# A state-space scan's sums: adding them to a PSUM bank that already holds the skip term

## The chip, the cores and the metric

The kernel runs on one core of one Trainium2 chip. Its time is the device time of one execution in microseconds (us), the median of several runs; the profile is of one further execution of the same program. A core has five engines, each of which works through its own instructions in program order: TensorE (PE, matmuls, with weight loads shown as PEld), VectorE (DVE), ScalarE (ACT), GpSimd (POOL) and SyncE (SP), which here only issues DMAs. Engines wait for each other through semaphores.

## The reference

The input is 8 images of 384 channels and 32 x 32 points. Layer 0 normalises each point, runs a Mamba block forwards and backwards over the 1024 points, and adds a gated depthwise convolution. Layer 1 is causal attention with 6 heads and a quantised feed-forward network with 1536 hidden units, applied to the first five images. What the change touches is the Mamba block's output, once for each direction:

```python
def step(h, inp):
    dA, dBu, c = inp
    h = dA * h + dBu
    return (h, jnp.einsum('bdn,bn->bd', h, c))
...
y = ys.transpose(1, 0, 2) + u * D_param
y = y * silu(z)
return jnp.einsum('bld,od->blo', y, out_proj_w)
...
g = (fwd + bwd) * scale_mod
```

Each channel has 16 states. The recurrence runs over the points; the states are weighted with C and summed, the skip term u D is added, and the result is gated with z. Gate and output projection are linear in y and the same for both directions, so the kernel adds the two directions' y first and gates and projects once.

## The kernel before, in words

**Recording and planning.** Every instruction is recorded as an `Op` with its tiles, and a planner (`Plan.place`) lays out the order of all engines with a list schedule: each operation has an assumed duration (`Plan.cost`), is ready when what it depends on has ended, and of the ready ones of an engine the one with the lowest rank goes first, if its tiles have a free buffer. Rank is the place in the recording, less what `hurry` takes off: 600 for all work of the scan, 60 more where a block says so. Operations in a `together` block stay adjacent. The resulting order is emitted as one fixed program per engine, so an edit in one place can move instructions everywhere. Since one helper emits everything, all of them carry line 367 in the profile, and are told apart by tile names.

**The scan.** A unit is (image b, part, channel chunk c of 128, state group j of 4, half q). The four parts of an image are (direction, half of the points) = (0,0), (0,1), (1,1), (1,0); the last image has the two directions exchanged. For each part and chunk there are 4 x 2 = 8 units, here called a group: 96 units an image, 768 in all, in 96 groups. In a unit the 128 partitions are 32 channels by 4 states, and it covers two such blocks of 512 points:

- `s_load`, `s_row`: SP loads delta (`scan_dl`), delta times u (`scan_ud`), and the rows B and C (`scan_bc`), from DRAM, broadcast over partitions.
- `s_first`: POOL makes `g = ud * B`, 128x1024, in one of six buffers (`scan_g`).
- `s_scan`: for each block ACT makes `da = exp(A dl)` in one of two PSUM banks (`ps_da`), DVE runs the recurrence over `g` in place (TENSOR_TENSOR_SCAN); the last column is kept for the next half by ACT (`scan_carry`); then POOL multiplies `g` by C in place.
- `s_sum`: for each pair of units (q = 0 and 1) four matmuls with the constant `gather` add up the 4 states of each channel and write 32 partitions each of the one PSUM bank `y` (`ps_y`). Four pairs make a group; the first starts the sum (`start=True`), the last ends it. When the pair's matmuls are done, its `g` buffers are free.
- `s_gate`: closes a group. SP loads u (`scan_us`). In the direction that comes first, DVE writes `yt = u D + y` to SBUF (`scan_yt`). In the second, DVE does three operations: `y = u D + y`, `y = yt + y`, `z = z y`, with z loaded into `scan_z`; SP writes the result to DRAM (`dram_sp_gy`), from where the attention reads it.

Units are shifted against each other: in the slot of unit k, `s_load` and the B rows are for unit k + 4, `s_first` for k + 2, `s_scan` for k, and `s_sum` and `s_gate` for k - 1.

**Beside the scan.** The steps of the other stages (`before_scan` of coming images, `attention` and the feed-forward network of finished ones) fill the other engines between the scan's slots, spread over them by assumed costs and due times. After the last unit only the second half of the last image's attention is left. `ident` is an identity matrix, `wproj` a weight of the attention, `vec` holds per-channel constants, D among them. PSUM has eight banks: one for `y`, two for `da`, five for everything else (`ps_any`).

Of the kernel before, what the change touches and what calls it, by code (L numbers as in the profile page):

```python
# [10 lines left out]
F32 = mybir.dt.float32  # L11
BF16 = mybir.dt.bfloat16
AF = mybir.ActivationFunctionType
ALU = mybir.AluOpType
# [4 lines left out]
P = 128  # L19
# [3 lines left out]
HB = 512  # L23
# [31 lines left out]
V_NORM, V_CW, V_CB, V_DTB, V_D, V_DW, V_DWB, V_BP, V_B2 = 0, 1, 5, 6, 7, 8, 17, 18, 19  # L55
# [105 lines left out]
class Plan:  # L161
# [15 lines left out]
    @contextmanager  # L177
    def together(self):
        self.group = []
        yield  # L180
        self.group = None

    @contextmanager
    def hurry(self, offset):
        self.sooner += offset
        yield
        self.sooner -= offset
# [193 lines left out]
def kernel(  # L381
# [21 lines left out]
    nc = plan = Plan(tc, homes)  # L403
    together, hurry = plan.together, plan.hurry
# [5 lines left out]
    sp = Pool(plan, "scan", 2, bass.MemoryType.SB)  # L410
# [3 lines left out]
    def ctile(name, shape, dt=F32):  # L414
        return const.tile(shape, dt, name=name, tag=name)
# [12 lines left out]
    def bank(name, tag=None):  # L428
        tag = tag if tag in BANKS else "any"
        return ps.tile([P, HB], F32, name=name, tag=tag, bufs=BANKS[tag])  # L430
# [4 lines left out]
    def half(h):  # L435
        return slice(h * HB, (h + 1) * HB)
# [4 lines left out]
    def load(dst, src):  # L441
        nc.sync.dma_start(out=dst, in_=src)
# [8 lines left out]
    spilled = {}  # L451
# [8 lines left out]
    vec = ctile("vec", [P, NC, NV])  # L460
# [8 lines left out]
    for d in range(2):  # L469
        nc.scalar.dma_start(out=wdt[d * DW : d * DW + RANK, :], in_=w_dt)  # L470
        nc.scalar.dma_start(
            out=wdt[d * DW + RANK : d * DW + RANK + 1, :],
# [10 lines left out]
    wproj = ctile("wproj", [P, NC, C])  # L483
    nc.scalar.dma_start(out=wproj, in_=w_proj.rearrange("(c p) e -> p c e", p=P))

    ident = ctile("ident", [P, P])
    make_identity(tc.nc, plan.now(ident))

    cmask = ctile("cmask", [P, HB], BF16)
    nc.vector.memset(cmask, 0.0)  # L490
# [468 lines left out]
    sst = {}  # L959
# [16 lines left out]
    def s_row(u, i):  # L976

        if u.c > 0 or u.q > 0:
            return
        r = sp.tile([P, HB], F32, name=f"bc{i}_{u.name}", tag=f"bc{i}", bufs=NG)  # L980
        rows = spilled[u.b, "rows", u.d][i * NS + u.j * SUB : i * NS + (u.j + 1) * SUB, half(u.h)]
        load(r, rows.partition_broadcast(BLK))
        sst["bc", i, u.b, u.part, u.j] = r
# [36 lines left out]
    def s_sum(u):  # L1020

        if u.q == 0:
            sst["pair"] = sst.pop(("g", u.name))
            return
        if u.j == u.first_group:
            sst["y"] = bank(f"y_{u.name}", "y")
        y = sst["y"]
        pair = (sst.pop("pair"), sst.pop(("g", u.name)))
        with together():
            for k in (2, 3, 0, 1):  # L1030
                nc.tensor.matmul(
                    out=y[k * BLK : (k + 1) * BLK, :],
                    lhsT=gather,
                    rhs=pair[k // 2][:, k % 2, :],
                    start=(u.j == u.first_group),
                    stop=(u.j == u.last_group),
                    skip_group_check=True,
                )

    def s_gate(u):  # L1040

        if not u.closes:
            return
        b, c, h, y = u.b, u.c, u.h, sst["y"]
        key = ("yt", b, c, h)
        t = sp.tile([P, HB], F32, name=f"uh_{u.name}", tag="us", bufs=1)
        load(t, spilled[b, "u", u.d, c][:, half(h)])
        if key not in sst:
            yt = sp.tile([P, HB], F32, name=f"yt_{u.name}", tag="yt", bufs=2 * NC)
            with hurry(offset=60):  # L1050
                nc.vector.scalar_tensor_tensor(
                    yt, t, vec[:, c, V_D : V_D + 1], y, ALU.mult, ALU.add
                )
            sst[key] = yt
            return
        z = sp.tile([P, HB], F32, name=f"zh_{u.name}", tag="z", bufs=1)
        load(z, spilled[b, "z", c][:, half(h)])
        yt = sst.pop(key)
        with hurry(offset=60):
            nc.vector.scalar_tensor_tensor(y, t, vec[:, c, V_D : V_D + 1], y, ALU.mult, ALU.add)  # L1060
            nc.vector.tensor_tensor(y, yt, y, ALU.add)
            nc.vector.tensor_tensor(z, z, y, ALU.mult)
        gy = dram.tile([P, HB], F32, name=f"sgy_{u.name}", tag=f"sp_gy_{c}_{h}")
        nc.sync.dma_start(out=gy, in_=z)
        spilled[b, "gy", c, h] = gy
# [440 lines left out]
    def slots(lo, hi):  # L1506
        def at(f, k):
            if 0 <= k < len(units):
                f(units[k])

        def slot(k):
            at(s_load, k + AHEAD + 2)
            at(lambda u: s_row(u, 0), k + AHEAD + 2)
            at(lambda u: s_row(u, 1), k + 2)
            at(s_first, k + AHEAD)
            at(s_scan, k)
            at(s_sum, k - 1)
            at(s_gate, k - 1)

        def ahead_of_all(k):  # L1520
            with hurry(offset=600):
                slot(k)

        return [(lambda k=k: ahead_of_all(k), 5.0) for k in range(lo, hi)]
# [62 lines left out]
    at = 0.0  # L1587
# [61 lines left out]
```

## Time and profile before

| what | value |
|---|---|
| time, median of 3 runs | 4044.43 us (4044.12 to 4044.86) |
| the profiled execution | 4048.24 us |
| its span, first to last instruction | 4046.4 us |
| TensorE's granted clock, mean over the span | 0.90 |
| busy: POOL, PE, DVE, ACT | 3570.8, 3387.3, 3264.4, 2546.6 us |
| first and last scan product on POOL start at | 74.8 and 3858.9 us |
| `ps_y` matmul records, DVE closings | 3072; 192 |
| ACT table loads | 131 |

The page is read as follows. The busy line gives each engine's busy time, its share of the span and its number of instruction records; an fp32 matmul is recorded as two. The slices cut the span into 40 equal parts of 101 us, and a digit is the busy share in tenths. A group's line has: source line, engine, operation, output tile <- input tiles, shape, xcount | busy us, mean ns of one | idle us of the engine just before them, and what ended that idle time. A line of waits reads: engine and what it was about to write <- whose end released it: us in total, times, the longest. A line of the timeline has start us, duration us, engine, operation, tiles, and in brackets the idle time before it. Buffer numbers are left out of names.

### The profile page before, as it was taken

The numbers are of one execution on the slowest core, as the hardware profiler recorded it, in microseconds if no ns is written. First come the engines' busy times: TensorE is split into PE (matmuls) and PEld (weight loads), VectorE is DVE, ScalarE is ACT, GpSimd is POOL, SyncE is SP. The second block draws the span as 40 slices with busy tenths as digits, with TensorE's granted clock in tenths as the row PEclk, the third lists the DMA queues.
The fourth block names the chain that finished last, engine by engine and source line by source line (L and its number), as shares of the span: only waits on it lengthen the run. The fifth ranks groups of instructions, "written<-read, shape, count | busy, mean of one in ns | idle before, by whom it ended". The sixth has DMA issues, their size and how long they took to land. (4 is left out here: it accounts for less than half of the span.)

```text
span 4046.4 us, 42961 instructions
## 1 busy us (share of the span) xinstructions
PE 3387.3 (84%) x12426; PEld 1330.0 (33%) x12426; DVE 3264.4 (81%) x4580; ACT 2546.6 (63%) x4967; POOL 3570.8 (88%) x1559
## 2 busy tenths in 40 slices
PE   5585679888699897998986989969989699898899
PEld 1121223333134332343332333323433233333344
DVE  5888987889977899678897687996779977778843
ACT  5666665866746766547667377664676654847635
POOL 2999999999999999789998799987899997999910
PEclk8685779899799898899997999979999799999999
DMA  7547655343563344742445533446334473333300
GB/s 237 194 141 242 235 191 174 100 144 126 202 209 124 102 147 135 247 157 86 134 161 195 183 110 105 138 169 242 123 100 138 142 266 127 113 122 108 128 16 32
DMA packets 338965, 611.99 MB, mean 151 GB/s; under 512 B 34616, under 2 KB 93416, under 8 KB 338728
## 3 DMA queue, kind: packets, MB, share of 16 engines
q1 hardware_dynamic: 329072, 593.10, 43.3%
q10 hardware_dynamic: 9656, 16.15, 1.2%
q8 instruction: 98, 1.61, 0.2%
q14 instruction: 139, 1.14, 0.1%
HBM read 456.03 MB, written 153.09 MB: 151 GB/s over the span
## 5 line engine op out<-in xcount | busy, mean ns | idle before, releaser
L367 POOL TENSOR_TENSOR scan_g<-scan_ud,scan_bc 128x1024 f32<-128x1024 f32 x768 | 1815.9, 2369 | 164.7 <-PE ps_y L367 97.0
L367 POOL TENSOR_TENSOR scan_g<-scan_g,scan_bc 128x1024 f32<-128x1024 f32 x768 | 1816.6, 2369 | 120.9 <-ACT scan_carry L367 66.0
L367 ACT ACTIVATE ps_da<-scan_dl,const_amat 128x512 f32<-128x512 f32 x1536 | 1052.6, 691 | 813.7 <-DVE scan_g L367 800.6
L367 DVE TENSOR_TENSOR_SCAN scan_g<-ps_da,scan_carry,scan_g 128x512 f32<-128x512 f32 x768 | 940.0, 1267 | 111.1 <-POOL scan_g L367 88.0
L367 PE MATMUL ps_any<-big_big,mid_mid 128*128 128x512 f32 x2016 | 952.9, 625 | 78.4 <-DVE big_big L367 56.5
L367 DVE TENSOR_TENSOR_SCAN scan_g<-ps_da,scan_g 128x512 f32<-128x512 f32 x768 | 893.1, 1206 | 127.8 <-POOL scan_g L367 86.9
L367 PE MATMUL ps_y<-scan_g,const_gather 128*32 128x512 f32 x3072 | 467.8, 686 | 275.1 <-POOL scan_g L367 265.0
L367 PEld LDWEIGHTS ps_any<-big_big,mid_mid 128*128 128x128 f32 x2016 | 388.0, 199 | 662.9 <-issue 486.3
L367 PE MATMUL ps_any<-big_big,big_big 128*128 128x512 f32 (+4 forms) x1728 | 551.9, 558 | 15.9 <-DVE small_nm L367 5.3
L367 PE MATMUL ps_any<-const_ident,mid_mid 128*128 128x128 f32 x1728 | 309.4, 304 | 96.0 <-DVE small_nm L367 44.1
L367 DVE CUSTOM_DVE_ANT_0 mid_mid<-ps_any,const_cmask 128x512 f32<-128x512 f32 (+3 forms) x576 | 291.2, 546 | 70.7 <-PE ps_any L367 69.7
L367 PEld LDWEIGHTS ps_any<-big_big,big_big 64*128 64x128 f32 (+1 forms) x1728 | 223.1, 189 | 309.9 <-issue 199.0
L367 DVE SCALAR_TENSOR_TENSOR ps_any<-big_big,const_vec,ps_any 128x496 f32<-128x496 f32 (+6 forms) x420 | 303.1, 727 | 21.6 <-ACT ps_any L367 11.9
L367 PEld LDWEIGHTS ps_any<-const_ident,mid_mid 128*128 128x128 f32 x1728 | 197.9, 149 | 331.2 <-DVE small_nm L367 100.3
L367 ACT COPY ptp_ptn<-ps_any 128x512 f32<-128x512 f32 (+3 forms) x576 | 255.2, 478 | 47.3 <-PE ps_any L367 38.4
L367 PE MATMUL ps_any<-ptp_ptn,big_big 128*64 128x512 f32 (+3 forms) x1152 | 262.3, 536 | 14.6 <-ACT ptp_ptn L367 13.1
L367 ACT ACTIVATE mid_mid<-mid_mid,small_low 128x512 f32<-128x512 f32 (+3 forms) x384 | 242.3, 634 | 47.5 <-DVE small_low L367 47.5
L367 PEld LDWEIGHTS ps_y<-scan_g,const_gather 128*32 128x32 f32 x3072 | 64.2, 114 | 545.0 <-POOL scan_g L367 443.6
L367 PE MATMUL ps_any<-mid_mid,const_onesc 128*128 128x512 f32 x252 | 131.2, 655 | 60.5 <-ACT mid_mid L367 45.6
L367 ACT ACT_TABLE_LOAD x131 | 168.1, 1283 | 2.9 <-PEq L1636 0.7
L367 PE MATMUL ps_any<-mid_mid,const_wdt 25*128 25x512 f32 x192 | 132.1, 852 | 41.6 <-DVE mid_mid L367 32.2
L367 DVE COPY big_big<-ps_any 128x512 f32<-128x512 f32 (+1 forms) x86 | 54.2, 631 | 128.6 <-PE ps_any L367 128.6
(100 smaller groups left out, 3185.4 us busy)
## 6 DMA issues: line engine op xcount, KB each, us to landing
scan_dl<-dram_sp_dl SPq DMA_DIRECT2D x384, 256.0 KB, 3.3
scan_ud<-dram_sp_ud SPq DMA_DIRECT2D x384, 256.0 KB, 3.7
scan_bc<-dram_rows SPq DMA_DIRECT2D x256, 256.0 KB, 3.4
scan_us<-dram_sp_u SPq DMA_DIRECT2D x96, 256.0 KB, 2.7
mid_mid<-dram_sp_u SPq DMA_DIRECT2D x96, 256.0 KB, 4.9
dram_sp_dl<-mid_mid SPq DMA_DIRECT2D x96, 256.0 KB, 4.0
dram_sp_ud<-mid_mid SPq DMA_DIRECT2D x96, 256.0 KB, 4.6
dram_sp_u<-mid_mid SPq DMA_DIRECT2D x42, 512.0 KB, 4.9
```

Source lines behind the costliest of these rows:

```text
L367: getattr(engine, what)(*[mapped(v) for v in args], **{k: mapped(v) for k, v in kwargs.items()})
```

## The change

The u load moves into a step of its own, `s_skip`, four units ahead of the scan, with two buffers in place of one. A new step `s_seed`, placed between `s_scan` and `s_sum`, takes the bank `y` and has ACT write `u D` to it; in the second direction DVE then adds `yt` to it in place. All sums are now accumulated on this content (`start=False`); a single matmul at the program's start writes the whole bank once, so that later matmuls without a start flag add to what is there. Closing a group is now one operation: in the first direction ACT copies `y` to `yt`, in the second DVE multiplies z by `y`.

```diff
+    nc.tensor.matmul(
+        out=bank("written", "y"),
+        lhsT=ident,
+        rhs=wproj.rearrange("p c e -> p (c e)")[:, :HB],
+        start=True,
+        stop=True,
+    )
...
-        if u.j == u.first_group:
-            sst["y"] = bank(f"y_{u.name}", "y")
...
-                    start=(u.j == u.first_group),
+                    start=False,
...
+    def s_skip(u):
+
+        if not u.opens:
+            return
+        t = sp.tile([P, HB], F32, name=f"uh_{u.name}", tag="us", bufs=2)
+        load(t, spilled[u.b, "u", u.d, u.c][:, half(u.h)])
+        sst["us", u.b, u.c, u.part] = t
+
+    def s_seed(u):
+
+        if not u.opens:
+            return
+        t, y = sst.pop(("us", u.b, u.c, u.part)), bank(f"y_{u.name}", "y")
+        yt, scale = sst.pop(("yt", u.b, u.c, u.h), None), vec[:, u.c, V_D : V_D + 1]
+        with hurry(offset=60):
+            nc.scalar.activation(y, t, AF.Copy, scale=scale)
+            if yt is not None:
+                nc.vector.tensor_tensor(y, yt, y, ALU.add)
+        sst["y"], sst["second"] = y, yt is not None
+
     def s_gate(u):
...
-        key = ("yt", b, c, h)
-        t = sp.tile([P, HB], F32, name=f"uh_{u.name}", tag="us", bufs=1)
-        load(t, spilled[b, "u", u.d, c][:, half(h)])
-        if key not in sst:
+        if not sst["second"]:
             yt = sp.tile([P, HB], F32, name=f"yt_{u.name}", tag="yt", bufs=2 * NC)
             with hurry(offset=60):
-                nc.vector.scalar_tensor_tensor(
-                    yt, t, vec[:, c, V_D : V_D + 1], y, ALU.mult, ALU.add
-                )
-            sst[key] = yt
+                nc.scalar.copy(yt, y)
+            sst["yt", b, c, h] = yt
             return
...
-        yt = sst.pop(key)
         with hurry(offset=60):
-            nc.vector.scalar_tensor_tensor(y, t, vec[:, c, V_D : V_D + 1], y, ALU.mult, ALU.add)
-            nc.vector.tensor_tensor(y, yt, y, ALU.add)
             nc.vector.tensor_tensor(z, z, y, ALU.mult)
...
             at(s_first, k + AHEAD)
+            at(s_skip, k + 4)
             at(s_scan, k)
+            at(s_seed, k - 1)
             at(s_sum, k - 1)
             at(s_gate, k - 1)
```

## The prediction

> **What bounds the kernel now.** First the page's busy times and its slices.
>
> ```profile
> PE 3387.3 (84%) x12426; PEld 1330.0 (33%) x12426; DVE 3264.4 (81%) x4580; ACT 2546.6 (63%) x4967; POOL 3570.8 (88%) x1559
> POOL 2999999999999999789998799987899997999910
> ```
>
> GpSimd (POOL) leads, and is full from its start at 74.8 us to the last scan unit at 3863 us; the head before and the tail after hold none of its work. Inside it is not full everywhere: the slices with 7 and 8 lie in the second half. So the span is head 75, POOL's work, POOL's waits, tail 183. Next the groups of instructions, each shape apart, for POOL and for what the change touches.
>
> ```profile
> L367 POOL TENSOR_TENSOR scan_g<-scan_ud,scan_bc 128x1024 f32<-128x1024 f32 x768 | 1815.9, 2369 | 164.7 <-PE ps_y L367 97.0 <-DMA scan_ud<-dram_sp_ud 61.5 <-issue 4.8
> L367 POOL TENSOR_TENSOR scan_g<-scan_g,scan_bc 128x1024 f32<-128x1024 f32 x768 | 1816.6, 2369 | 120.9 <-ACT scan_carry L367 66.0 <-DVE scan_g L367 42.6 <-issue 3.6
> L367 DVE SCALAR_TENSOR_TENSOR ps_y<-scan_us,const_vec,ps_y 128x512 f32<-128x512 f32 x48 | 35.9, 747 | 27.2 <-PE ps_y L367 27.0
> L367 DVE SCALAR_TENSOR_TENSOR scan_yt<-scan_us,const_vec,ps_y 128x512 f32<-128x512 f32 x48 | 35.5, 740 | 27.9 <-PE ps_y L367 27.7
> L367 DVE TENSOR_TENSOR ps_y<-scan_yt,ps_y 128x512 f32<-128x512 f32 x48 | 33.4, 696 | 1.6
> L367 DVE TENSOR_TENSOR scan_z<-scan_z,ps_y 128x512 f32<-128x512 f32 x48 | 33.0, 686 | 1.6
> L367 ACT ACTIVATE ps_any<-mid_mid,const_vec 128x512 f32<-128x512 f32 x60 | 40.9, 684 | 0.1
> L367 ACT COPY mid_mid<-ps_any 128x512 f32<-128x512 f32 x234 | 129.9, 584 | 36.8 <-PE ps_any L367 31.3 <-DVE mid_mid L367 3.6 <-DVE big_big L367 1.2
> ```
>
> A unit costs POOL 2 x 2.36 = 4.7 us and a group of eight 37.8 us; none of it is edited. What can move is its idle time of 285.5 us: 61.5 in the head, 224 inside. Of the inside, 97.0 is the first product waiting for a `g` buffer that TensorE's sums still hold; 66.0 and 42.6 are the second product waiting for carry or scan. The waits by stretch of POOL (75 to 1600 us, then 2150 to 2350 us) say where:
>
> ```profile
> POOL scan_g L367 <- PE ps_y L367: 3.4, 1, 3.4
> ...
> POOL scan_g L367 <- PE ps_y L367: 24.2, 5, 9.6
> ```
>
> The same question for 1600-1860, 2690-2880 and 3220-3420 us gives 22.8, 27.8 and 18.4. So 93.2 of the 97.0 us fall in four stretches, one in each of the batches 4 to 7. The timeline around 1700 us shows how one arises.
>
> ```profile
> 1698.40 1.06 PE L367 MATMUL ps_y<-scan_g,const_gather 128*32 128x512 f32 x8
> 1699.40 20.87 PE L367 MATMUL ps_any<-big_big,mid_mid 128*128 128x512 f32 x48
> 1720.19 1.07 PE L367 MATMUL ps_y<-scan_g,const_gather 128*32 128x512 f32 x8
> ...
> 1721.37 4.69 POOL L367 TENSOR_TENSOR scan_g<-scan_ud,scan_bc 128x1024 f32<-128x1024 f32 x2 [7.57 <-PE ps_y L367]
> ```
>
> TensorE works in program order; 24 matmuls (two records each, 0.87 us a matmul) stand between two sums, POOL uses up its six buffers and waits 7.57 us. What sets the loss is how unevenly the planner lays other work between the sums.
>
> **The change part by part.**
>
> *VectorE.* Two multiply-adds go: 48 x 0.747 + 48 x 0.740 = 71.4 us. The add of `yt` (0.696) and the product with z (0.686) stay, 48 each; the add moves ahead of the sums. VectorE falls to 3193 us.
>
> *ScalarE.* It gains 96 seeds `y <- D u`; nearest row: SBUF to PSUM with a scale of one value per partition, 0.684 us, so 65.7; and 48 copies `yt <- y`, by the PSUM-to-SBUF row 0.584, 28.0. Together 93.7: 2640 us, 65%. Table loads stay 131. Against this stands the Trainium skill, "ScalarE: Activation LUTs", Rules for kernel authors: for multiplies and adds use VectorE, not ScalarE. The rows first: at 128x512 fp32 ScalarE's 0.684 and 0.584 are below VectorE's 0.747 and 0.740; the page's ground, VectorE up to about 3x faster, is for bf16. By the rows ScalarE's larger sum comes only from 48 more instructions; by the rule, if each took 3 x 0.74 = 2.2 us, ScalarE would gain 144 x 2.2 = 317 us and stand at 2864, still under POOL. I go by the rows. The cover is ScalarE's idle time: its exponentials wait 800.6 us in all for VectorE's scans to free a bank. Without it 93.7 us would count in full.
>
> *TensorE.* The sums keep their shape, only the start flag goes. One matmul is added at the start, so that the bank counts as written. The skill's "PSUM — Partial Sum Buffer" (Summary: rules for kernel authors) says that an accumulation seeded by ScalarE or VectorE must have seed 0, any other going through TensorE. No row shows such a seed. By the rule 96 identity matmuls x 0.87 = 84 us of PE work would be due; with the one priming matmul it is 1.0 us. Breaking it would give wrong sums, not a longer time, so I charge 1.0. That matmul stands second on TensorE and waits for `wproj` (issued at 10.4 us, landed 12.7 later, at 23.1); behind it on TensorE stand the first norm's sums, which started at 24.6 us before: 0 to 1 us late.
>
> *Loads on SyncE (SP).* 96 loads of u remain, with two buffers, issued earlier. A load waits for its buffer: before, for VectorE's closing; now for a seed on ScalarE, with the queue standing behind it in both. At the very start the third u load stands before the eight `scan_bc` loads, which began at 54.0 us; it waits for the first seed, which by its place follows an activation that ended at 54.5 and takes 0.7. Those loads slip 1.6 us, hidden until the `dram_sp_dl` writes at 60.4, which themselves slip 0.7, as Softplus stands behind the seed. **Head: +1 us** (0 to 2).
>
> *The bank's turn.* One bank `y` serves all 96 groups. Before: last sum, closing, first sum of the next. After: last sum, closing, seed, for 48 groups also the add, first sum. First direction: 0.58 + 0.68 = 1.27 against 0.74; second: 0.69 + 0.68 + 0.70 = 2.07 against 2.13, but over three hand-overs between engines (some 0.1 us each by the gaps between dependent rows) and with up to five queued VectorE rows between z's product and the add. Behind a seed that waits, exponentials stand on ScalarE; behind the copy as well, which takes over VectorE's 27.7 us wait for TensorE. Matching the records group by group, the next group's first product pair is done a median 4.8 us after the old closing's end, so most turns are hidden; 10 of 95 had no slack, 7 more under 2 us. Bounds: 0 (the six buffers, 9.4 us of POOL work, cover all) to some 40 us (some 15 turns at 2.7). I take **+11 us**, nearer the lower end, since before the change TensorE's sums waited 0.8 us for `scan_z` and 7.3 us, once, for another VectorE row, though half of the closings lasted 2 us.
>
> *The order.* Fewer VectorE and more ScalarE instructions change the planner's whole layout. I count, in each program's order, TensorE's other work between consecutive sums at 0.87 us per 512 columns, and add up what exceeds 9.4 us, a pair of units on POOL. Before, batches 1 to 8: 1, 11, 16, 65, 62, 58, 64, 26 us. After: 3, 9, 15, 19, 55, 44, 56, 26. The count finds the four stretches in which POOL waited, which supports it. There 249 us of excess gave 93.2 us of wait, 0.37 each; the after has 155 in three batches, so 58, and batch 4 with 19 resembles batches 2 and 3, so 2. **PE waits: 93 to 60, -33 us** (bounds -60 to +10, the ratio per batch being 0.29 to 0.48 and the layout untried). In batch 4 the run of VectorE work between two scans, 24 us around 1607-1627 us, where POOL waited 9.7 us, is now split into two of about 11; the split form, in batch 3, cost 2.4 + 3.4 = 5.8: **-4**.
>
> *The tail.* 183 us, same TensorE work behind the last sum; the final closing is one operation instead of three: **-1**.
>
> Sum: -33 - 4 + 11 + 1 - 1 = -26. The profiled execution took 4048.2 us (span 4046.4 and 1.8 around it), 3.8 above the median of the runs. 4048.2 - 26 - 3.8 = **4018 us**.
>
> **Rivals.** *The turn bites (slower).* In the three remaining stretches the buffers are used up, and a late seed there holds TensorE with everything behind it, and POOL through it. For: a sequence over three engines, each in order, some with an 11.1 us Gelu block on ScalarE. Against: the median slack of 4.8 us. It outweighs the gain of 37 once turns cost over about 37 us, 0.4 us on each of 95; at 0.6 us each, 57 us, the time is 4044 - 37 + 57 = 4064. *Waits change their name (no change).* The room that the more even order gives is taken by carry and scan waits (108.6 us now), as ScalarE is fuller by 94 us: 4044 - 26 + 25 = 4043. *VectorE's relief counts too.* If those 108.6 us shrink by a quarter as VectorE loses 71 us and its bunches get smaller: 4018 - 27 = 3991; for: the same count, VectorE's work above 3.6 us between scans, falls from 256 to 209 us; against: most of those waits are Gelu stretches on ScalarE.
>
> **How the numbers follow.** Forecast 0.45; relief as well 0.15; no change 0.12; the turn bites 0.28. A difference of 0.2%, 8 us, is about what can be told from none. Faster: 0.45 + 0.15 = 0.60; within: 0.12; slower: 0.28. The range, 3988 to 4064, leaves out the turn's worst and deepest relief; the forecast's own is 4000 to 4036.
>
> **What would show it.** Right: POOL's wait for `ps_y` near 70 us, none over 3 us between 1660 and 1860 us; POOL's busy time unchanged; seeds near 0.68 and copies near 0.58 us; few waits of TensorE's sums for a seed or the add. Wrong: a total over 110 us there, sums waiting for ACT or DVE `ps_y` by tens of us, or carry waits well over 66.

## The result, and the profile after

The changed kernel takes 3992.93 us (3992.03 to 3994.79, four runs) against 4044.27 us (4042.36 to 4044.86, four runs): the ratio is 0.9874, with a 95% interval of 0.9857 to 0.9892. It is 51 us faster; 26 had been forecast. The profiled span is 3990.2 us, 56.2 less than before.

First the busy line and POOL's slices of the kernel after:

```profile
PE 3390.6 (85%) x12428; PEld 1334.1 (33%) x12428; DVE 3197.7 (80%) x4481; ACT 2627.6 (66%) x5114; POOL 3574.2 (90%) x1559
POOL 2999999999999999999998799988999879999910
```

POOL is as busy as before (3574 against 3571 us), VectorE has 66.7 us less, ScalarE 81.0 more. The slices below 9 that stood at 1620-1820 us are gone; those of the later stretches remain.

The groups of instructions, each shape apart, for POOL and the operations on the bank `y`:

```profile
L367 POOL TENSOR_TENSOR scan_g<-scan_ud,scan_bc 128x1024 f32<-128x1024 f32 x768 | 1822.5, 2377 | 126.4 <-DMA scan_ud<-dram_sp_ud 62.6 <-PE ps_y L367 55.7 <-issue 8.0
L367 POOL TENSOR_TENSOR scan_g<-scan_g,scan_bc 128x1024 f32<-128x1024 f32 x768 | 1820.0, 2373 | 101.2 <-ACT scan_carry L367 55.5 <-DVE scan_g L367 40.6 <-POOL scan_g L367 1.9
L367 ACT ACTIVATE ps_y<-scan_us,const_vec 128x512 f32<-128x512 f32 x96 | 66.1, 689 | 38.0 <-DVE scan_z L367 37.1
L367 DVE TENSOR_TENSOR scan_z<-scan_z,ps_y 128x512 f32<-128x512 f32 x48 | 32.7, 682 | 22.9 <-PE ps_y L367 22.7
L367 DVE TENSOR_TENSOR ps_y<-scan_yt,ps_y 128x512 f32<-128x512 f32 x48 | 32.6, 680 | 4.8 <-ACT ps_y L367 4.8
L367 ACT COPY scan_yt<-ps_y 128x512 f32<-128x512 f32 x48 | 27.9, 582 | 23.1 <-PE ps_y L367 22.9
```

POOL's idle time is 227.6 us, of which 62.6 in the head: inside the scan it waits 165.0 us, against 224.0 before. The 59.0 us between, less 3.4 us of longer POOL work, are the whole gain of the span; head (+0.9) and tail (-1.6) nearly cancel. Of the 59, 41.3 are waits for the sums (97.0 to 55.7) and 12.5 waits for carry and scan (108.6 to 96.1). The waits by stretch of POOL, the sums' line for 1560-1860 us (batch 4) and then for 2110-2310 (batch 5):

```profile
POOL scan_g L367 <- PE ps_y L367: 2.9, 2, 1.7
...
POOL scan_g L367 <- PE ps_y L367: 22.5, 6, 7.6
```

For 2640-2830 and 3160-3370 us it is 14.4 and 13.4. So batches 4 to 7 went from 22.8, 24.2, 27.8 and 18.4 to 2.9, 22.5, 14.4 and 13.4: 53 us in all, where the count of TensorE's work between sums had said 60, with batch 4 nearly free of waits. In the list of waits, the new hand-overs at the bank:

```profile
ACT ps_y L367 <- DVE scan_z L367: 37.1, 22, 5.4
...
PE ps_y L367 <- DVE ps_y L367: 3.0, 1, 3.0
```

TensorE's sums waited for a seed or add once, for 3.0 us. What remains of the turn lies on ScalarE, whose seeds waited 37.1 us for the product with z to free the bank.

### The profile page after: what moved, and what is told of

Its sections match the earlier page's. It is cut to its first block, busy times and chain, and to the rows that moved or that the text cites. A ratio compares the mean times of both kernels' runs of the same rounds, so it can differ in the third digit from the quotient of the medians.

```text
span 3990.2 us, 43097 instructions
## 1 busy us (share of the span) xinstructions
PE 3390.6 (85%) x12428; PEld 1334.1 (33%) x12428; DVE 3197.7 (80%) x4481; ACT 2627.6 (66%) x5114; POOL 3574.2 (90%) x1559
## 5 line engine op out<-in xcount | busy, mean ns | idle before, releaser
L367 POOL TENSOR_TENSOR scan_g<-scan_ud,scan_bc 128x1024 f32<-128x1024 f32 x768 | 1822.5, 2377 | 126.4 <-DMA scan_ud<-dram_sp_ud 62.6
L367 POOL TENSOR_TENSOR scan_g<-scan_g,scan_bc 128x1024 f32<-128x1024 f32 x768 | 1820.0, 2373 | 101.2 <-ACT scan_carry L367 55.5
L367 PE MATMUL ps_any<-big_big,big_big 128*128 128x512 f32 (+4 forms) x1728 | 548.0, 559 | 14.4 <-DVE big_big L367 5.6
L367 ACT ACTIVATE mid_mid<-mid_mid,small_low 128x512 f32<-128x512 f32 (+3 forms) x384 | 242.5, 634 | 46.9 <-DVE small_low L367 46.6
L367 ACT COPY mid_mid<-ps_any 128x512 f32<-128x512 f32 x234 | 130.0, 584 | 35.9 <-PE ps_any L367 31.3
```

The lines of the kernel that those rows point to most:

```text
L367: getattr(engine, what)(*[mapped(v) for v in args], **{k: mapped(v) for k, v in kwargs.items()})
```

## The experiments

Theory 1: the gain is the planner's order, more even because the planner knows of lighter VectorE work. Theory 2: the gain is VectorE's relief itself, in whatever order. "The count" is the prediction's: TensorE's work beyond 9.4 us between sums, over batches 4 to 7; 249 us before, 174 after. It is taken from the planned order, not measured. A price is a change of the time for each us by which an engine's busy time changed.

**Relief alone, in the order of before.** Both kinds of multiply-add are planned at full cost and issued on 8 of 512 columns; most of the skip term and of the first direction's result is left out. (POOL also zeroes the six `yt` buffers at the start, 2.9 us in the head.)

```diff
-                nc.vector.scalar_tensor_tensor(
-                    yt, t, vec[:, c, V_D : V_D + 1], y, ALU.mult, ALU.add
-                )
+                with plan.eight_columns():
+                    nc.vector.scalar_tensor_tensor(
+                        yt, t, vec[:, c, V_D : V_D + 1], y, ALU.mult, ALU.add
+                    )
...
```

> The kernel before, in its own order and with its own plan, but the 96 multiply-adds that take in the skip term work on 8 columns of 512 (the skip term and the first direction's result are left out but for these columns), so VectorE loses about 60 us and the bank's turn gets some 0.6 us shorter. If the gain of the change is the order that the planner makes (theory 1): POOL's wait for the sums stays near 97 us, time 4036 to 4044. If the gain is VectorE's relief itself, whatever the order (theory 2): about 4044 - 40 = 4004, at least below 4020.

Measured 4026.02 us against 4046.23: ratio 0.9957 (0.9935 to 0.998), -20 us. The busy line, then POOL's waits:

```profile
PE 3383.7 (84%) x12426; PEld 1330.4 (33%) x12426; DVE 3218.9 (80%) x4580; ACT 2547.8 (63%) x4967; POOL 3572.4 (89%) x1565
```

```profile
POOL scan_g L376 <- PE ps_y L376: 96.3, 23, 12.5
...
POOL scan_g L376 <- ACT scan_carry L376: 51.9, 37, 7.4
```

Between the two theories. The waits for the sums stayed (97.0 to 96.3), as theory 1 said; but 45.5 us less on VectorE took 14 us off the waits for the carry, and 20 off the time, 0.44 us per us. Relief has a price of its own. (The turn also got 0.5 us shorter; the waits for the sums show nothing of it.)

**Order alone, without relief.** Every instruction of before; the planner counts nothing for the multiply-adds.

```diff
-        cost = self.cost(name, what, args, kwargs, written, views)
+        cost = 0.0 if self.hidden else self.cost(name, what, args, kwargs, written, views)
...
-            nc.vector.scalar_tensor_tensor(y, t, vec[:, c, V_D : V_D + 1], y, ALU.mult, ALU.add)
+            with plan.other_cost():
+                nc.vector.scalar_tensor_tensor(y, t, vec[:, c, V_D : V_D + 1], y, ALU.mult, ALU.add)
```

> The kernel before with every instruction, but the planner counts nothing for the 96 multiply-adds, so it lays out an order as if VectorE had been relieved. TensorE's work over 9.4 us between sums falls from 249 to 200 us in batches 4 to 7 (batch 4: 65 to 34). Theory 1: 4044 - 0.4 to 0.7 x 49, 4010 to 4024, batch 4's waits mostly gone. Theory 2: no relief, 4040 to 4050.

Measured 4036.11 us, ratio 0.9975 (0.9965 to 0.9984), -10 us, less than either end of theory 1. Busy line and POOL's waits:

```profile
PE 3389.9 (84%) x12426; PEld 1333.1 (33%) x12426; DVE 3263.3 (81%) x4583; ACT 2544.9 (63%) x4964; POOL 3573.5 (89%) x1559
```

```profile
POOL scan_g L373 <- ACT scan_carry L373: 78.8, 50, 10.2
...
POOL scan_g L373 <- DVE scan_g L373: 62.6, 39, 10.9
...
POOL scan_g L373 <- PE ps_y L373: 60.7, 19, 9.6
```

The count was right on the sums: 97.0 to 60.7, batch 4 from 22.8 to 5.4. But carry and scan waits rose from 108.6 to 141.4: this order, made for a lighter VectorE than there is, gave back most of what it won.

**Both together.** Narrowed multiply-adds and no cost for them in the plan (the lines are against the narrowed kernel above):

```diff
-        cost = self.cost(name, what, full, kwargs, written, views)
+        cost = 0.0 if self.narrow else self.cost(name, what, args, kwargs, written, views)
```

> Narrowed multiply-adds (8 of 512 columns, the rest of the skip term and of the first direction's result left out) in the order that the planner makes when it counts nothing for them. If order and relief add up: 4036 - 20 = 4016. If the order gains only when VectorE is in fact relieved, as the scan waits that it brought suggest: 3990 to 4005.

Measured 4007.90 us against 4044.12, ratio 0.9907 (0.9878 to 0.9936), -36. The busy line:

```profile
PE 3375.9 (84%) x12426; PEld 1328.8 (33%) x12426; DVE 3216.4 (80%) x4583; ACT 2547.6 (64%) x4964; POOL 3577.3 (89%) x1565
```

Relief in this order is worth 28.2 us (4036.1 to 4007.9) for 46.9 us of VectorE, 0.60 per us: more than in the order of before. The gain beyond the 4016 of plain addition, 8 us, is smaller than the interval's half width of 12, so it is not shown that the two do more than add.

**VectorE's work put back in the order of after.** Two multiply-adds of 256 columns behind the last scan of each group, unseen by the planner:

```diff
+                if u.closes and i == 1:
+                    with plan.unplanned():
+                        for _ in range(2):
+                            nc.vector.scalar_tensor_tensor(
+                                spare, spare, vec[:, u.c, V_D : V_D + 1], spare, ALU.mult, ALU.add
+                            )
```

> The changed kernel in its own order, with the work of the 96 removed multiply-adds put back on VectorE as two idle multiply-adds of 256 columns after the last scan of each group, which the planner does not see. Theory 1 (the order): 3993 to 4003. Theory 2 (the relief): some 4030 to 4044, as the 71 us are back.

Measured 4325.36 us against the changed kernel's 3992.93, +332 us, outside both expectations. The group of the added instruction, shape apart:

```profile
L376 DVE SCALAR_TENSOR_TENSOR const_spare<-const_spare,const_vec 128x256 f32<-128x256 f32 x192 | 493.1, 2568 | 3.4
```

An instruction of 0.46 us at its shortest took 2.57 us on average and up to 11.6. It read two operands from SBUF (where the `const_` and `scan_` tiles lie) while POOL's products ran at their usual 2380 and 2377 ns; the removed multiply-adds had one operand in PSUM (where the `ps_` tiles lie). The pair with the longest one, and POOL beside it:

```profile
3840.28 2.38 POOL L376 TENSOR_TENSOR scan_g<-scan_ud,scan_bc 128x1024 f32<-128x1024 f32 x1
...
3840.56 12.09 DVE L376 SCALAR_TENSOR_TENSOR const_spare<-const_spare,const_vec 128x256 f32<-128x256 f32 x2
3842.60 2.36 POOL L376 TENSOR_TENSOR scan_g<-scan_g,scan_bc 128x1024 f32<-128x1024 f32 x1
...
3849.49 2.36 POOL L376 TENSOR_TENSOR scan_g<-scan_ud,scan_bc 128x1024 f32<-128x1024 f32 x1
```

The run's granted TensorE clock was also lower, 0.869 for 0.901; what share of the 332 us goes with that is not known. The run therefore prices no relief, and it was repeated with the bank `da` as the second operand:

```diff
-                                spare, spare, vec[:, u.c, V_D : V_D + 1], spare, ALU.mult, ALU.add
+                                spare, spare, vec[:, u.c, V_D : V_D + 1], da[:, : HB // 2], ALU.mult, ALU.add
```

> The changed kernel in its own order, VectorE given back the 96 multiply-adds' work as two of 256 columns after the last scan of each group, unseen by the planner, now with one operand in PSUM, as the removed ones had. If relief of 71 us is worth the 20 us that narrowing gave in the order of before: 4008 to 4018. If the more even order leaves room for it: 3993 to 4000. If the two SBUF operands were not what cost 330 us: again near 4300.

Measured 4026.05 us against 4044.12, ratio 0.9955 (0.9933 to 0.9978), and 33 us above the changed kernel, more than either relief at the price of the first experiment or free room had promised. The busy line, the same group, then POOL's waits:

```profile
PE 3397.1 (84%) x12428; PEld 1336.3 (33%) x12428; DVE 3276.9 (81%) x4673; ACT 2629.3 (65%) x5114; POOL 3575.5 (89%) x1560
L376 DVE SCALAR_TENSOR_TENSOR const_spare<-const_spare,const_vec,ps_da 128x256 f32<-128x256 f32 x192 | 89.9, 468 | 3.4
```

```profile
POOL scan_g L376 <- ACT scan_carry L376: 68.0, 43, 9.7
...
POOL scan_g L376 <- DVE scan_g L376: 56.4, 31, 9.7
```

468 ns each: it was the two SBUF operands. VectorE is 79.2 us busier than in the changed kernel, and the time rose by 33, 0.42 per us, 28.3 of it through carry and scan (96.1 to 124.4). That is an upper end, as the bank `da` is also held longer here (ScalarE waited 47.5 us for it). The more even order left no free room for the old work.

**ScalarE's work and the turn.** The seed written twice, unseen by the planner:

```diff
-            nc.scalar.activation(y, t, AF.Copy, scale=scale)
+            with together():
+                nc.scalar.activation(y, t, AF.Copy, scale=scale)
+                with plan.unplanned():
+                    nc.scalar.activation(y, t, AF.Copy, scale=scale)
```

> The changed kernel in its own order, each seed written twice by ScalarE, the second unseen by the planner: each of the 96 turns of the bank is 0.7 us longer and ScalarE has 66 us more. If turns are hidden (median slack): 3993 to 3999, and the turn of the prediction's sum was worth about 0, not 11. If turns reach POOL: 96 x 0.7 = 66 us at most, over 4015.

Measured 4016.07 us against 4046.23, ratio 0.9927 (0.9899 to 0.9956), +23 on the changed kernel: beyond the expectation for a hidden turn, and below 66. Against it, the same amount of ScalarE work outside the turn:

```diff
+                if u.closes and i == 1:
+                    with plan.unplanned():
+                        for _ in range(2):
+                            nc.scalar.activation(spare, spare, AF.Copy, scale=vec[:, u.c, V_D : V_D + 1])
```

> The changed kernel in its own order, with some 66 us of idle work on ScalarE, unseen by the planner, placed not in the bank's turn but behind the last exponential of each group. If the second seed cost 23 us because ScalarE is fuller: 4010 to 4020. If it was the longer turn of the bank: 3993 to 4000.

Measured 4003.63 us against 4044.12, ratio 0.9897 (0.9868 to 0.9925), +11, between its two expectations. POOL's waits with the seed doubled, then with the idle work on ScalarE:

```profile
POOL scan_g L376 <- ACT scan_carry L376: 63.5, 38, 8.8
POOL scan_g L376 <- DVE scan_g L376: 53.5, 28, 9.7
POOL scan_g L376 <- PE ps_y L376: 46.6, 12, 10.2
```

```profile
POOL scan_g L376 <- ACT scan_carry L376: 57.8, 36, 8.7
POOL scan_g L376 <- PE ps_y L376: 48.3, 15, 10.2
POOL scan_g L376 <- DVE scan_g L376: 43.2, 24, 9.7
```

ScalarE is 72.1 us busier in the second, for 10.7 us: 0.15 per us, from two runs. The doubled seed costs 23 for 61.0, so its place adds some 14. But POOL's waits for the sums did not grow in either. (They seem to fall, from 55.7 to 46.6 and 48.3, but in each run one wait at the same product, 6.5 and 7.6 us long, is put down to a DMA instead; with it they are 53.1 and 55.9.) With the seed doubled it is the waits for carry and scan that rose, from 96.1 to 117.0: a seed held up seems to reach POOL through the exponentials and scans behind it, not through the sums.

**The changed kernel, planned as if VectorE were not relieved.** The planner counts 0.643 us more for the last scan of each group; count 210.

```diff
-        cost = self.cost(name, what, args, kwargs, written, views)
+        cost = self.cost(name, what, args, kwargs, written, views) + (0.643 if self.hidden else 0.0)
```

> The changed kernel with every instruction as it is, but the planner counts 0.64 us more for the last scan of each group, about what it counted for the multiply-add, as if VectorE were not relieved. TensorE's work over 9.4 us between sums rises from 174 to 210 us in batches 4 to 7 (batch 4: 19 to 38). If the relief makes the better order: 4005 to 4020. If moving the skip term to the sum's start does, whatever VectorE's load: 3988 to 4000.

Measured 4015.06 us, ratio 0.9925 (0.9896 to 0.9954): 22 of the 51 us are lost by the plan's belief alone, with every instruction as in the changed kernel. POOL's wait for the sums is 68.8 us for 55.7, in batch 4 10.0 for 2.9, and carry and scan take 108.6 for 96.1:

```profile
POOL scan_g L373 <- PE ps_y L373: 68.8, 18, 10.2
...
POOL scan_g L373 <- ACT scan_carry L373: 57.8, 36, 10.2
POOL scan_g L373 <- DVE scan_g L373: 50.8, 19, 11.9
```

**One part alone: early loads of u.** `s_skip` is added as in the change, with its two buffers.

```diff
-        t = sp.tile([P, HB], F32, name=f"uh_{u.name}", tag="us", bufs=1)
-        load(t, spilled[b, "u", u.d, c][:, half(h)])
+        t = sst.pop(("us", u.b, u.c, u.part))
...
+            at(s_skip, k + 4)
```

> The kernel before with one part of the change: u is loaded four units ahead into two buffers. No engine is relieved. The count falls from 249 to 225 us by the new order: 4028 to 4046. If late loads of u had been part of the waits: below 4025.

Measured 4035.18 us against 4044.89, ratio 0.9975 (0.9965 to 0.9985), -10, within the range that the count (225 for 249) gave. Late loads of u were at most a small part of the waits.

**The change with the seed on VectorE.**

```diff
-            nc.scalar.activation(y, t, AF.Copy, scale=scale)
+            nc.vector.tensor_scalar(y, t, scale, None, ALU.mult)
```

> The changed kernel with the seed y = D u written by VectorE instead of ScalarE, planned anew: some 60 us more on VectorE, 66 less on ScalarE. At 0.42 us per us of VectorE and 0.15 of ScalarE: +25 - 10; the count rises from 174 to 211 us, +15: about 4020, 4008 to 4032. If only the structure (seed first, one closing) matters: 3988 to 4000.

Measured 4033.78 us, ratio 0.9973 (0.996 to 0.9987). Busy line, and the one line of POOL's waits that stands out:

```profile
PE 3386.3 (84%) x12428; PEld 1333.0 (33%) x12428; DVE 3262.4 (81%) x4583; ACT 2573.3 (64%) x5012; POOL 3571.2 (89%) x1559
```

```profile
POOL scan_g L367 <- PE ps_y L367: 88.0, 22, 11.9
```

A little outside the expectation's upper end. With VectorE as busy as before, seeding the sum and closing in one operation bring 11 us, no more than the lower count (211 for 249) is worth in the table below. In this form TensorE's sums waited 15.0 us for VectorE's seed or add, against 3.0 in the change. So the structure alone does not make the gain; it needs the work taken off VectorE.

**Another order for both kernels.** The planner's cost of a POOL product is set to 2.35 us, near the 2.36 of the profile, instead of 2.31. No instruction changes, only their order.

```diff
-            return 0.05 + n * 0.00221
+            return 0.05 + n * 0.00225
```

> The kernel before with the same edit of the planner's cost of POOL. Its count over batches 4 to 7 falls from 249 to 174 us, that of the changed kernel; VectorE's from 222 to 168. If unevenness alone made the gain of the change: about 3993 to 4000. If VectorE's relief counts for some 28 us besides and ScalarE's load costs 12: 4005 to 4015.

> The changed kernel, every instruction the same; the planner counts a POOL product at 0.00225 us an element instead of 0.00221 (2.35 us instead of 2.31; the profile has 2.36), which makes another order. TensorE's work over 9.4 us between sums falls from 174 to 127 us in batches 4 to 7, VectorE's over 3.6 us between scans from 175 to 139. If unevenness sets the waits, at 0.4 to 0.5 us per us: 3993 - 19 to 24, 3967 to 3977. If not: 3985 to 4000.

Measured 4018.07 us for the kernel before with this edit (0.9932, 0.9912 to 0.9951), a little above what was expected, and 3972.78 us for the changed one (0.9819, 0.9802 to 0.9835), as expected: 20 us below the change and the fastest of all. POOL's waits in the first, and its wait for the sums in the second:

```profile
POOL scan_g L367 <- ACT scan_carry L367: 79.3, 43, 8.4
...
POOL scan_g L367 <- DVE scan_g L367: 51.2, 30, 9.1
POOL scan_g L367 <- PE ps_y L367: 46.4, 15, 8.4
```

```profile
POOL scan_g L367 <- PE ps_y L367: 33.6, 11, 7.7
```

All kernels but those with added work, by the count and VectorE's busy time; VectorE has its old load in the upper half and is relieved in the lower:

| kernel | count, us | VectorE busy, us | POOL's wait for sums | for carry and scan | time, us |
|---|---|---|---|---|---|
| before | 249 | 3264 | 97.0 | 108.6 | 4044 |
| loads of u early | 225 | 3274 | 78.5 | 113.2 | 4035 |
| change, seed on VectorE | 211 | 3262 | 88.0 | 99.7 | 4034 |
| before, multiply-adds not counted | 200 | 3263 | 60.7 | 141.4 | 4036 |
| before, POOL counted at 2.35 us | 174 | 3264 | 46.4 | 130.5 | 4018 |
| before, multiply-adds narrowed | 249 | 3219 | 96.3 | 93.3 | 4026 |
| change, planned as unrelieved | 210 | 3196 | 68.8 | 108.6 | 4015 |
| before, narrowed and not counted | 200 | 3216 | 59.1 | 116.9 | 4008 |
| change | 174 | 3198 | 55.7 | 96.1 | 3993 |
| change, POOL counted at 2.35 us | 127 | 3187 | 33.6 | 101.8 | 3973 |

The columns of waits go by the releaser named; in the last row one more wait of a second product, 11.9 us, is put down to a DMA.

Within each half of the table the time falls with the count, by 0.35 us per us in the upper ((4044 - 4018) / 75) and 0.43 in the lower ((4026 - 3973) / 122); two neighbours with nearly the same count differ by a few us. At equal or nearly equal counts the relieved kernels are 18 to 28 us faster. Two cautions: the lower half mixes narrowed kernels with changed ones, whose ScalarE is some 80 us busier; and the count is not the only thing that a new order moves. The same kind of count for VectorE's work between scans fell as well with POOL at 2.35 us (222 to 168 before, 175 to 139 in the change), so a slope belongs to the order as a whole, not to TensorE's part alone.

## Why the prediction was right, and where it was short

The direction and the wide range held. The forecast's own range, 4000 to 4036, did not: 3993 lies where the rival "VectorE's relief counts too" had put it, at 3991. That this fits to 2 us is in part luck, since the rival had it from a turn of 11 us, a ScalarE at nothing, and carry and scan waits 27 us shorter, of which 12.5 came.

The main step, **the order**, did what it said: -33 us of waits for the sums were forecast and -41 seen, batch 4 at 2.9 us for a forecast 2. Its worth in time can be read on the way from before, over the kernel before with the same count (174), to the change: the first half is the order alone, 26 us, at the table's two slopes 26 to 32; forecast with the Gelu stretch were 37. There the waits for the sums fell by 50.6 us, but those for carry and scan rose by 21.9 (108.6 to 130.5).

The step that failed is the one on **VectorE**: "VectorE falls to 3193 us" was a statement with no price in the sum, and the relief stood only as a rival at 0.15, worth 27 us. It happened: narrowing in the order of before gave 20 us, and the price found three times is 0.42 to 0.60 us for a us, which makes 28 to 40 us of 66.7. The second half of the way, at equal count, gave 25 us with ScalarE's added load in it, and there carry and scan waits fell from 130.5 to 96.1. The argument against relief, that these waits are mostly Gelu stretches on ScalarE, was wrong by a good part: POOL's wait for the carry fell (66.0 to 51.9) when VectorE alone got lighter. ScalarE's copy of the carry does wait for VectorE's scan, 110.3 us before; but that total stayed at 109.6 in the narrowed kernel, so the path in detail is not shown.

**ScalarE** was priced at nothing under cover of its waits. At 0.15 us per us, its 81 us cost about 12. By the durations the prediction chose rightly: a seed took 0.689 us on ScalarE and 0.744 on VectorE, a copy 0.582, and none came near the 2.2 us of its other reckoning. **The turn** was priced at 11 us; on TensorE's side it came to 3.0 us of waits. What the 37.1 us that seeds waited on ScalarE cost beside that was not measured by itself; that a turn can cost is shown by the doubled seed, whose place added some 14 us. The sums on a seeded bank were no slower, 679 ns a record for 686.

So the two errors on ScalarE and the turn nearly cancel, and the 25 us between forecast and result are relief, less what the order fell short. An estimate that closes: order 26, ScalarE's 12 against it, and 37 left for relief, 0.56 us per us, within the 0.42 to 0.60 found apart; at the lowest price relief is 28 and the order 35. The split is known to some 10 us, not better.

Of the rivals, "the turn bites" fell with the 3.0 us. "Waits change their name" did occur in an order made without relief (-10 us instead of some 20), not in the change. Head (+0.9 for a forecast +1) and tail (-1.6 for -1) held, though POOL's last product before ended at 3861.3 us, not 3863, so that the tail was 185 us.

What stays open is how much of the more even order is due to a lighter VectorE. Where the planner was told of less VectorE work, or less of it was there, the count fell: 249 to 200, 210 to 174, 174 to 127. But every new plan of the kernel before had a lower count than its own 249, and a changed cost of POOL's products brought it to 174 with no relief at all. In part the order of before may have been an unlucky one; no run takes the planner apart.

## What to carry to other kernels

Where one engine paces the work and the others feed it in a fixed order, price relief of a feeding engine even if it is busy only 80%: find the waits of the pacing engine that pass through it, and take a price per us from an experiment that narrows instructions in an unchanged order. Where a planner writes the order, count the work that stands between the feeding instructions before trusting any sum of durations; here that count ranked the kernels well enough to find a further 20 us in a 2% change of one planner cost. An edit that moves work between engines should be planned anew with costs that fit it: here the plan for the old load cost the changed kernel 22 of its 51 us.

## What the runs showed of the hardware

The 128x256 multiply-add on VectorE took 468 ns with one operand in SBUF and one in PSUM, and 2568 ns on average, 11.6 us at most, with both in SBUF beside POOL's products; 192 of them cost 332 us of time in one case and 33 in the other. In the slow case 155 of the 192 took longer than 0.52 us, 475.4 us together, and for 474.7 of these POOL was at work on a product; of the 37 short ones 30 met no product at all. The longest lasted through the ends of five products in a row. POOL's own products did not lengthen (2380 and 2377 ns for 2377 and 2373 in the changed kernel). The Trainium skill states the rule in "SBUF — State Buffer", section Who interferes with whom: "A DVE instruction with two SBUF inputs contends with a GpSimd instruction that reads SBUF". The trace agrees, and shows the price where POOL is nearly always busy: here VectorE alone waited, for up to five POOL products. In this kernel the removed multiply-adds, the add of `yt` and the product with z all have one operand in PSUM, and took 0.68 to 0.75 us.
